# An LSTM with a residual on one core: the last block of h Wh is multiplied by halves of the columns, and the output gate's sigmoid is made by halves

## The chip, the cores and the metric

One Trainium2 chip, one of its cores. The metric is the device time of one execution in microseconds (us); lower is better. TensorE (PE in the profile) does the matrix products, with its weight loads shown apart as PEld; VectorE is DVE, ScalarE is ACT, GpSimd is POOL, and SyncE (SP) issues DMA transfers.

## The reference

An LSTM over 512 time steps for 32 sequences, with 512 inputs and 512 hidden units, in float32; its hidden states are added to its input.

```python
xW = jnp.einsum('ntd,dg->ntg', x, Wx) + b
def step(carry, xw_t):
    prev_h, prev_c = carry
    a = xw_t + prev_h @ Wh                 # [32, 2048]
    i = jax.nn.sigmoid(a[:, :Hd])
    f = jax.nn.sigmoid(a[:, Hd:2 * Hd])
    o = jax.nn.sigmoid(a[:, 2 * Hd:3 * Hd])
    g = jnp.tanh(a[:, 3 * Hd:])
    next_c = f * prev_c + i * g
    next_h = o * jnp.tanh(next_c)
    return ((next_h, next_c), next_h)
...
return x + hs
```

The products `prev_h @ Wh` depend on the step before; the products x Wx don't.

## The kernel before

**Layout.** The 2048 gate columns are cut into four groups j of 512 columns, and the 32 sequences of group j lie on partitions 32j to 32j+31. So one PSUM bank of 128 partitions by 512 columns (2 KB a partition) holds all gates of one step. Within a group the 512 columns are two halves of 256 columns, and a half holds 64 hidden units ("u" in `cell`) with their four gates. A hidden unit's gates all lie in the same half.

**One step.** `h_part(t)` adds h Wh to the step's bank `gbank[t % 2]`, into which the input part was copied before (`seed_step`, L585). The 512 rows of Wh are four blocks k of 128; for each k and each j there is one matmul of 128 x 32 weights (h of block k) by 128 x 512 columns (Wh), 16 in all. A float32 matmul is two instructions on TensorE, so the profile counts 32 for a step. `cell(t)` then makes the gates on ScalarE and the state on VectorE. For each half it computes a sigmoid of two gates (L225, 128 columns) and a tanh (L226, 64 columns); the output gate's sigmoid follows once for both halves (L227, 128 columns). VectorE makes the products (L229) and the new c (L230) of each half; ScalarE makes tanh c (L232); VectorE makes h (L234) and transposes it into the form that the next step's matmuls take as weights (L236). Blocks k = 0 and 1 of the next step need the first half of the units, and k = 2 and 3 the second.

**What stands beside it.** The x Wx of steps 24 to 503 is computed for groups of 24 steps by a fast matrix product: 20 smaller products of seven parts, that is 140 parts of 4 matmuls with 256 columns for 24 steps (`emit_matmuls`, L477). Their results are summed in `evacuate` and `w_op` on ScalarE and VectorE. These matmuls are emitted behind `h_part(t)` and fill TensorE while `cell(t)` runs; 140 parts over 24 steps makes 6 parts in 20 of the steps and 5 parts in four. For the first 20 steps, and for the last ones, plain products x Wx (`plain_block`, L159) fill in.

**The last steps.** From step 478 on (`SPLIT`), `is_split(t)` holds: the two halves of a step stand in two banks (`PAIRS`), every matmul of `h_part` is by halves of 256 columns, and `cell` goes through the halves one after the other, with an output sigmoid of 64 columns in each.

**Order.** Each engine takes its instructions in the order in which the code emits them (`manual_schedule`); a tile framework adds the waits on semaphores. Every step emits `h_part(t)`, then loads and copies, then the filling matmuls, then `cell(t)`.

Of the kernel before, what the change touches and what calls it, by code (L numbers as in the profile page):

```python
# [8 lines left out]
AF = mybir.ActivationFunctionType  # L9
# [6 lines left out]
NJ = 4  # L16
# [72 lines left out]
def kernel(  # L89
# [10 lines left out]
    nc = tc.nc  # L100
# [40 lines left out]
    def x_of(t):  # L141
        return xnat[:, xslot(t // TC), t % TC]
# [45 lines left out]
    def is_split(t):  # L188
        return t >= SPLIT

    def bank_of(t):
        if t < KEPT:
            return [gbank[0], gbank[1], xbank[3], xbank[4], xbank[0]][t]
        return gbank[t % 2]

    def half_of(t, i):
        if is_split(t):
            return PAIRS[t % 2][i][:, 0:HW]
        return bank_of(t)[:, i * HW : (i + 1) * HW]

    def h_part(t):
        if is_split(t):
            order = [(i, k) for i, ks in ((0, (0, 1)), (1, (0,)), (0, (2, 3)), (1, (1, 2, 3))) for k in ks]
        else:
            order = [(None, k) for k in range(NJ)]
        for i, k in order:
            dst = bank_of(t) if i is None else half_of(t, i)
            for j in range(NJ):
                m = wh_sb[:, k, j] if i is None else wh_sb[:, k, j, i * HW : (i + 1) * HW]
                nc.tensor.matmul(  # L210
                    dst[j * B : (j + 1) * B], state["ht"][:, k], m, start=False, stop=True, skip_group_check=True
                )

    def cell(t):
        n, tt = divmod(t, TC)
        s, nxt = sring[t % 2], sring[(t + 1) % 2]
        o = oring[0]
        ht = htr[t % 2]
        by_gate = lambda a: a.rearrange("p (h g u) -> p h g u", g=G, u=H)
        for part in [(0,), (1,)] if is_split(t) else [(0, 1)]:  # L220
            i = slice(part[0], part[-1] + 1)
            units = slice(H * part[0], H * (part[-1] + 1))
            g = by_gate(half_of(t, part[0])) if is_split(t) else by_gate(bank_of(t))
            for n_, u in enumerate(part):
                nc.scalar.activation(s[:, u, 0:2], g[:, n_, 0:2], AF.Sigmoid)  # L225
                nc.scalar.activation(s[:, u, 2], g[:, n_, 3], AF.Tanh)  # L226
            nc.scalar.activation(o[:, i], g[:, :, 2], AF.Sigmoid)  # L227
            for u in part:
                nc.vector.tensor_mul(prod[:, u], s[:, u, 0:2], s[:, u, 2:4])  # L229
                add(nxt[:, u, 3], prod[:, u, 0], prod[:, u, 1])  # L230
            for u in part:
                nc.scalar.activation(tanh_c[:, HALVES[u]], nxt[:, u, 3], AF.Tanh)  # L232
            for u in part:
                nc.vector.tensor_mul(hbuf[:, HALVES[u]], o[:, u], tanh_c[:, HALVES[u]])  # L234
                if t < T - 1:
                    nc.vector.transpose(ht[:, 2 * u : 2 * u + 2].rearrange("p q b -> p (q b)"), hbuf[:, HALVES[u]])  # L236
            if t == T - 1:
                add(tanh_c[:, units], hbuf[:, units], x_last[:, units])
                nc.sync.dma_start(out=out[n][:, tt * P + units.start : tt * P + units.stop], in_=tanh_c[:, units])
        if t == T - 1:  # L240
            return
        state["ht"] = ht
        oc = ocr[t // 2 % 2]
        (nc.gpsimd if t < T - 8 else nc.vector).tensor_add(oc[:, tt % 2], x_of(t), ht)  # L244
        if tt % 2 == 1 or t == T - 2:
            m = tt % 2 + 1
            stores.append(
                lambda: nc.sync.dma_start(
                    out=out[n][:, (tt + 1 - m) * P : (tt + 1) * P],
                    in_=oc[:, 0:m].rearrange("p t q b -> p (t q b)"),  # L250
                )
            )
            if t == T - 2:
                stores.pop()()
# [463 lines left out]
    with tc.manual_schedule():  # L718
# [57 lines left out]

        for t in range(T):
            h_part(t)
            for f in stores + kept_stores:
                f()  # L780
# [18 lines left out]
            if t < HEAD_STEPS:  # L799
# [17 lines left out]
                for i, (kind, m) in enumerate(chunks):  # L817
                    if kind == "plain":
# [4 lines left out]
                        if i == 0:  # L823
                            cell(t)
                            if t + 1 >= KEPT:
                                seed_step(t + 1)
                            flush_v()
# [6 lines left out]
                    else:  # L834
# [13 lines left out]
                        if i == 0:  # L848
                            cell(t)
                            seed_step(t + 1)  # L850
                            flush_v()
                            if t == plains_done + 1:
                                load_seeds(((0, 0), (1, 1), (2, 2)), nc.gpsimd)
# [26 lines left out]
            g = group_loaded - 1  # L880
# [11 lines left out]
            for _ in range(0 if t < SPLIT - 2 else 2 if t < SPLIT else 1):  # L892
                if plain_tail:
                    p, c = plain_tail.pop(0)
                    plain_block(HEAD + NG * GS + p, c, tail_banks[p % 2])
                    if c == 3:
                        kept_late.append(p)
            cell(t)
            for p in kept_late:
                dst = cbuf[:, take(free_c), 0:2].rearrange("p s c -> p (s c)")  # L900
# [54 lines left out]
```

## Time and profile before

| | us |
|---|---|
| median of 3 runs | 3151.49 |
| lowest and highest | 3150.75, 3151.80 |
| span of the profiled execution, first to last instruction | 3148.0 |
| median less that span (start and end around the instructions) | 3.5 |
| TensorE busy in that span | 3119.0 |
| VectorE, ScalarE, GpSimd busy | 2232.8, 1454.6, 235.6 |

The span is that of one execution under the profiler; only the span is known of it, so the 3.5 us around it is taken from the median. A timeline row gives the start, the length of a run of like instructions, the engine, the line, the tiles, the shape and the count; in brackets stand the idle time before it and what ended it. Lengths of TensorE rows reach to the modelled end of the last matmul, and matmuls overlap: the pace of TensorE is read from one row's start to the next row's start.

### The profile page before, as it was taken

The numbers are of one execution on the slowest core, as the hardware profiler recorded it, in microseconds if no ns is written. First come the engines' busy times: TensorE is split into PE (matmuls) and PEld (weight loads), VectorE is DVE, ScalarE is ACT, GpSimd is POOL, SyncE is SP. The second block draws the span as 40 slices with busy tenths as digits, with TensorE's granted clock in tenths as the row PEclk, the third lists the DMA queues.
The fourth block names the chain that finished last, engine by engine and source line by source line (L and its number), as shares of the span: only waits on it lengthen the run. The fifth ranks groups of instructions, "written<-read, shape, count | busy, mean of one in ns | idle before, by whom it ended". The sixth has DMA issues, their size and how long they took to land.

```text
span 3148.0 us, 105007 instructions
## 1 busy us (share of the span) xinstructions
PE 3119.0 (99%) x41944; PEld 1616.1 (51%) x41944; DVE 2232.8 (71%) x6217; ACT 1454.6 (46%) x5481; POOL 235.6 (7%) x511
## 2 busy tenths in 40 slices
PE   9899999999999999999999999999999999999998
PEld 6544555555555555555555555555555555555465
DVE  5687777767676777777776767777777768677644
ACT  1244444444444444444444444444444444444444
POOL 0000000000000000000000000000000000000000
PEclk9999999999999999999999999999999999999999
DMA  8888777777877777777778777777777777777831
GB/s 290 286 284 269 241 257 243 248 256 247 262 226 254 249 260 241 259 241 249 257 244 265 231 249 251 261 243 251 243 253 257 245 259 231 250 255 235 270 94 37
DMA packets 310808, 766.66 MB, mean 244 GB/s; under 512 B 49392, under 2 KB 92144, under 8 KB 309808
## 3 DMA queue, kind: packets, MB, share of 16 engines
q1 hardware_dynamic: 296800, 740.82, 71.9%
q10 hardware_dynamic: 13280, 18.35, 1.6%
q8 instruction: 331, 5.42, 0.7%
q14 instruction: 157, 1.29, 0.1%
q0 software_dynamic: 240, 0.79, 0.1%
HBM read 577.04 MB, written 182.71 MB: 241 GB/s over the span
## 4 chain that ended last, share of the span: by engine, by line
PE 94%; DVE 3%; DMA 2%; issue 1%; ACT 1%; SPq 0%; POOL 0%; DVEq 0%; ACTq 0%; POOLq 0%
PE gbank L210 52%; PE xbank L477 31%; PE bbank L477 5%; PE xbank L159 2%; PE xbank L210 2%; DVE cbuf L353 1%; PE bbank L159 1%; DMA r<-in_L_cond_Wx_dram 0%; DMA xw<-xwd 0%; DMA xs<-in_L_cond_Wx_dram 0%; DVE prod L229 0%; DVE ubuf L388 0%; DMA vring<-vdram 0%; DVE s L230 0%; DMA r<-in_L_cond_b_dram 0%
## 5 line engine op out<-in xcount | busy, mean ns | idle before, releaser
L210 PE MATMUL gbank<-wh_sb,ht 128*32 128x512 f32 (+1 forms) x16288 | 1792.7, 579 | 6.9 <-DVE ht L236 2.3
L210 PEld LDWEIGHTS gbank<-wh_sb,ht 128*32 128x32 f32 x16288 | 615.0, 110 | 905.7 <-issue 727.1
L477 PE MATMUL xbank<-vring,ubuf 128*32 128x256 f32 x14400 | 932.8, 379 | 10.7 <-DVE ubuf L388 5.9
L225 ACT ACTIVATE s<-gbank 128x128 f32<-128x128 f32 x984 | 275.9, 281 | 1291.5 <-PE gbank L210 1270.9
L477 PEld LDWEIGHTS xbank<-vring,ubuf 128*32 128x32 f32 x14400 | 560.7, 110 | 377.0 <-issue 179.1
L229 DVE TENSOR_TENSOR prod<-s 128x128 f32<-128x128 f32 x1024 | 293.8, 287 | 648.6 <-ACT s L226 648.1
L353 DVE TENSOR_TENSOR cbuf<-cbuf 128x1024 f32<-128x1024 f32 x480 | 581.2, 1218 | 3.9
L244 POOL TENSOR_TENSOR oc<-xnat,ht 128x128 f32<-128x128 f32 x504 | 233.7, 464 | 2874.3 <-DVE ht L236 1601.3
L232 ACT ACTIVATE tanh_c<-s 128x64 f32<-128x64 f32 x1024 | 262.0, 257 | 278.8 <-DVE s L230 273.6
L236 DVE STREAM_TRANSPOSE ht<-hbuf 128x64 f32<-128x64 f32 x1022 | 250.8, 245 | 74.4 <-DVE hbuf L234 0.9
L585 ACT COPY gbank<-xw 128x512 f32<-128x512 f32 x473 | 284.1, 601 | 0.1
L230 DVE TENSOR_TENSOR s<-prod 128x64 f32<-128x64 f32 x1024 | 230.2, 225 | 35.3
L523 ACT COPY cbuf<-xbank 128x512 f32<-128x512 f32 x400 | 233.8, 585 | 40.8 <-PE xbank L477 27.2
L234 DVE TENSOR_TENSOR hbuf<-o,tanh_c 128x64 f32<-128x64 f32 x1024 | 213.2, 208 | 27.2 <-ACT tanh_c L232 26.1
L226 ACT ACTIVATE s<-gbank 128x64 f32<-128x64 f32 x984 | 226.6, 230 | 0.0
L533 DVE TENSOR_TENSOR cbuf<-xbank,cbuf 128x256 f32<-128x256 f32 x400 | 164.0, 410 | 79.0 <-ACT cbuf L532 74.8
L477 PE MATMUL bbank<-vring,ubuf 128*32 128x256 f32 x2400 | 192.3, 379 | 0.6 <-DVE cbuf L529 0.6
L477 PE MATMUL xbank<-vring,xs 128*32 128x256 f32 x2400 | 172.3, 381 | 0.8 <-DVE cbuf L533 0.5
L477 PE MATMUL xbank<-vring,r 128*32 128x256 f32 x2400 | 171.6, 379 | 0.1
L529 DVE TENSOR_TENSOR cbuf<-bbank,cbuf 128x256 f32<-128x256 f32 x400 | 162.0, 405 | 2.7 <-PE bbank L477 2.7
L536 DVE TENSOR_TENSOR cbuf<-xbank,cbuf 128x256 f32<-128x256 f32 x400 | 162.5, 406 | 0.0
L539 ACT COPY cbuf<-xbank 128x256 f32<-128x256 f32 x400 | 145.3, 363 | 20.4 <-PE xbank L477 11.1
(84 smaller groups left out, 1585.4 us busy)
## 6 DMA issues: line engine op xcount, KB each, us to landing
vring<-vdram SPq DMA_DIRECT2D x340, 896.0 KB, 5.9
xwd<-cbuf SPq DMA_DIRECT2D x240, 512.0 KB, 7.1
xw<-xwd SPq DMA_DIRECT2D x1920, 64.0 KB, 3.7
out_dram<-oc SPq DMA_DIRECT2D x255, 128.0 KB, 2.8
xnat<-in_x_dram SPq DMA_DIRECT2D x63, 512.0 KB, 5.0
xs<-in_x_grouped_dram SPq DMA_DIRECT2D x10, 1536.0 KB, 10.6
vring<-vdram SPq DMA_DIRECT2D x20, 768.0 KB, 6.6
r<-in_x_grouped_dram SPq DMA_DIRECT2D x10, 1536.0 KB, 10.3
```

Source lines behind the costliest of these rows:

```text
L210: nc.tensor.matmul(dst[j * B : (j + 1) * B], state["ht"][:, k], m, start=False, stop=True, skip_group_check=True)
L225: nc.scalar.activation(s[:, u, 0:2], g[:, n_, 0:2], AF.Sigmoid)
L226: nc.scalar.activation(s[:, u, 2], g[:, n_, 3], AF.Tanh)
L229: nc.vector.tensor_mul(prod[:, u], s[:, u, 0:2], s[:, u, 2:4])
L230: add(nxt[:, u, 3], prod[:, u, 0], prod[:, u, 1])
L232: nc.scalar.activation(tanh_c[:, HALVES[u]], nxt[:, u, 3], AF.Tanh)
L236: nc.vector.transpose(ht[:, 2 * u : 2 * u + 2].rearrange("p q b -> p (q b)"), hbuf[:, HALVES[u]])
L244: (nc.gpsimd if t < T - 8 else nc.vector).tensor_add(oc[:, tt % 2], x_of(t), ht)
L353: op(c_of(dst), c_of(src), c_of(bb))
L477: nc.tensor.matmul(dst[q * B : (q + 1) * B], left_of(gr, s, r)[:, q * B : (q + 1) * B], vring[:, row % 3, RIGHT[r]], start=start, stop=Tru ...
L523: nc.scalar.copy(t[:, 0:4:3], xb.rearrange("p (n c) -> p n c", n=2))
L585: nc.scalar.copy(bank_of(t), src)
```

## The change

Two edits. In `h_part`, for all steps before the split, the last block k = 3 is no longer four matmuls of 512 columns, but eight of 256: first the first halves of the four groups j, then the second halves. All go to the same bank as before. In `cell`, the output gate's sigmoid stands inside the loop over the halves, behind the tanh of its half, with 64 columns each time. In the split steps each part holds one half, so both edits leave these as they are.

```diff
@@ h_part
         else:
-            order = [(None, k) for k in range(NJ)]
+            order = [(None, k) for k in range(NJ - 1)] + [(i, NJ - 1) for i in range(2)]
         for i, k in order:
             dst = bank_of(t) if i is None else half_of(t, i)
@@ cell
         for part in [(0,), (1,)] if is_split(t) else [(0, 1)]:
-            i = slice(part[0], part[-1] + 1)
             units = slice(H * part[0], H * (part[-1] + 1))
             g = by_gate(half_of(t, part[0])) if is_split(t) else by_gate(bank_of(t))
             for n_, u in enumerate(part):
                 nc.scalar.activation(s[:, u, 0:2], g[:, n_, 0:2], AF.Sigmoid)
                 nc.scalar.activation(s[:, u, 2], g[:, n_, 3], AF.Tanh)
-            nc.scalar.activation(o[:, i], g[:, :, 2], AF.Sigmoid)
+                nc.scalar.activation(o[:, u], g[:, n_, 2], AF.Sigmoid)
```

How the instructions stand on an engine is shown below as the built program has it. A row gives the line, the operation, the tiles with the number of their buffer, the size and how many follow each other; in brackets are the semaphores for which the first of them waits, named by the engine or DMA queue that raises them. The changed file is one line shorter, so its L224, L225, L226 and L476 are L225, L226, L227 and L477 before.

TensorE in a step in the middle of the program, before (the step's 16 matmuls, and the fill behind them):

```order
L210 MATMUL gbank_0_72<-wh_sb_76,ht_1_95 32x512 [waits DVE_49,Activation_49]
L210 MATMUL gbank_0_72<-wh_sb_76,ht_1_95 32x512 x7
L210 MATMUL gbank_0_72<-wh_sb_76,ht_1_95 32x512 [waits DVE_49]
L210 MATMUL gbank_0_72<-wh_sb_76,ht_1_95 32x512 x7
L477 MATMUL xbank_2_68<-vring_77,ubuf_78 32x256 x4
```

The same step in the changed program:

```order
L210 MATMUL gbank_0_72<-wh_sb_76,ht_1_95 32x512 [waits DVE_49,Activation_49]
L210 MATMUL gbank_0_72<-wh_sb_76,ht_1_95 32x512 x7
L210 MATMUL gbank_0_72<-wh_sb_76,ht_1_95 32x512 [waits DVE_49]
L210 MATMUL gbank_0_72<-wh_sb_76,ht_1_95 32x512 x3
L210 MATMUL gbank_0_72<-wh_sb_76,ht_1_95 32x256 x8
L476 MATMUL xbank_2_68<-vring_77,ubuf_78 32x256 x4
```

The last four matmuls of 512 columns are eight of 256; no wait is added or moved, and the fill follows as before.

ScalarE in a step in the middle of the program, before (the copy of the next step's input part, the gates, tanh c, and a copy of the fill's results):

```order
L585 COPY gbank_1_73<-xw_83 128x512 [waits DMAHW6_49,DMAHW1_49,DMAHW7_49,DMAHW0_49,Activation_49]
L225 ACTIVATE s_0_88<-gbank_0_72 128x128 [waits PE_49]
L226 ACTIVATE s_0_88<-gbank_0_72 128x64
L225 ACTIVATE s_0_88<-gbank_0_72 128x128
L226 ACTIVATE s_0_88<-gbank_0_72 128x64
L227 ACTIVATE o_0_90<-gbank_0_72 128x128 [waits DVE_49]
L232 ACTIVATE tanh_c_92<-s_1_89 128x64 [waits DVE_49,Activation_49] x2
L532 COPY cbuf_75<-xbank_0_66 128x256 [waits PE_49]
```

The same place in the changed program:

```order
L584 COPY gbank_1_73<-xw_83 128x512 [waits DMAHW6_49,DMAHW1_49,DMAHW7_49,DMAHW0_49,Activation_49]
L224 ACTIVATE s_0_88<-gbank_0_72 128x128 [waits PE_49]
L225 ACTIVATE s_0_88<-gbank_0_72 128x64
L226 ACTIVATE o_0_90<-gbank_0_72 128x64 [waits DVE_49]
L224 ACTIVATE s_0_88<-gbank_0_72 128x128
L225 ACTIVATE s_0_88<-gbank_0_72 128x64
L226 ACTIVATE o_0_90<-gbank_0_72 128x64 [waits DVE_49]
L231 ACTIVATE tanh_c_92<-s_1_89 128x64 [waits DVE_49,Activation_49] x2
L531 COPY cbuf_75<-xbank_0_66 128x256 [waits PE_49]
```

One output sigmoid has moved up between the halves, and there is one instruction more. The first sigmoid of the step waits for TensorE; the sigmoid of the second half (the second L224) has no wait of its own in either program.

ScalarE in a split step, the same in both programs (rows of the program before):

```order
L225 ACTIVATE s_0_88<-xbank_0_66 128x128 [waits PE_49]
L226 ACTIVATE s_0_88<-xbank_0_66 128x64
L227 ACTIVATE o_0_90<-xbank_0_66 128x64
L232 ACTIVATE tanh_c_92<-s_1_89 128x64 [waits DVE_49]
L225 ACTIVATE s_0_88<-xbank_1_67 128x128 [waits PE_49]
```

Nothing moved here: the halves lie in two banks (`xbank_0` and `xbank_1`), and the sigmoid of each half waits for TensorE by itself.

## The prediction

> **What bounds the kernel now.** I read the page's shares and its chain first, then a timeline of TensorE alone, then one of all engines over a single step.
>
> ```profile
> span 3148.0 us, 105007 instructions
> PE 3119.0 (99%) x41944; PEld 1616.1 (51%) x41944; DVE 2232.8 (71%) x6217; ACT 1454.6 (46%) x5481; POOL 235.6 (7%) x511
> PE 94%; DVE 3%; DMA 2%; issue 1%; ACT 1%; SPq 0%; POOL 0%; DVEq 0%; ACTq 0%; POOLq 0%
> PE gbank L210 52%; PE xbank L477 31%; PE bbank L477 5%; PE xbank L159 2%; PE xbank L210 2%; DVE cbuf L353 1%; PE bbank L159 1%; DMA r<-in_L_cond_Wx_dram 0%; DMA xw<-xwd 0%; DMA xs<-in_L_cond_Wx_dram 0%; DVE prod L229 0%; DVE ubuf L388 0%; DMA vring<-vdram 0%; DVE s L230 0%; DMA r<-in_L_cond_b_dram 0%
> ```
>
> TensorE is the bound, and L210, the line that is edited, is the largest piece of the chain. But "99% busy" hides something: a matmul's row lasts beyond the start of the next, so a short wait between two matmuls doesn't show as idle. The distance from one step's first L210 matmul to the next step's shows it:
>
> ```profile
> 1535.94 3.64 PE L210 MATMUL gbank<-wh_sb,ht 128*32 128x512 f32 x32
> 1539.37 1.51 PE L477 MATMUL xbank<-vring,ubuf 128*32 128x256 f32 x24
> 1540.67 0.64 PE L477 MATMUL bbank<-vring,ubuf 128*32 128x256 f32 x8
> 1541.10 0.64 PE L477 MATMUL xbank<-vring,ubuf 128*32 128x256 f32 x8
> 1541.72 3.64 PE L210 MATMUL gbank<-wh_sb,ht 128*32 128x512 f32 x32
> 1545.15 1.07 PE L477 MATMUL xbank<-vring,ubuf 128*32 128x256 f32 x16
> ...
> 1547.74 3.64 PE L210 MATMUL gbank<-wh_sb,ht 128*32 128x512 f32 x32
> ...
> 1571.84 3.64 PE L210 MATMUL gbank<-wh_sb,ht 128*32 128x512 f32 x32
> ```
>
> Five steps from 1541.72 to 1571.84 take 30.12 us, 6.024 each: 3.43 for L210 (1541.72 to 1545.15) and 2.59 for 48 fill instructions, with no gap. These long steps are bound by TensorE's pace. The step from 1535.94 to 1541.72 has only 40 fill instructions. They start at 1539.37, the last 8 at 1541.10, and 8 take 0.43 (1540.67 to 1541.10), so TensorE could go on at 1541.53; it goes on at 1541.72. In these short steps the cell comes 0.19 us too late. By the code 4 of 24 steps are short; of the 458 steps 20 to 477 that is about 76.
>
> What the wait in a short step consists of, in another one of the same kind:
>
> ```profile
> 1503.26 1.50 PE L477 MATMUL xbank<-vring,ubuf 128*32 128x256 f32 x24
> 1503.53 0.28 ACT L225 ACTIVATE s<-gbank 128x128 f32<-128x128 f32 x1 [2.35 <-PE gbank L210]
> 1503.70 0.22 ACT L226 ACTIVATE s<-gbank 128x64 f32<-128x64 f32 x1
> 1503.81 0.28 ACT L225 ACTIVATE s<-gbank 128x128 f32<-128x128 f32 x1
> 1503.95 0.29 DVE L229 TENSOR_TENSOR prod<-s 128x128 f32<-128x128 f32 x1 [0.77 <-ACT s L226]
> 1503.96 0.24 ACT L226 ACTIVATE s<-gbank 128x64 f32<-128x64 f32 x1
> 1504.07 0.31 ACT L227 ACTIVATE o<-gbank 128x128 f32<-128x128 f32 x1
> 1504.28 0.22 DVE L230 TENSOR_TENSOR s<-prod 128x64 f32<-128x64 f32 x1
> 1504.42 0.28 DVE L229 TENSOR_TENSOR prod<-s 128x128 f32<-128x128 f32 x1
> 1504.60 0.26 ACT L232 ACTIVATE tanh_c<-s 128x64 f32<-128x64 f32 x1 [0.22 <-DVE s L230]
> 1504.74 0.23 DVE L230 TENSOR_TENSOR s<-prod 128x64 f32<-128x64 f32 x1
> 1504.89 0.23 DVE L234 TENSOR_TENSOR hbuf<-o,tanh_c 128x64 f32<-128x64 f32 x1
> 1505.22 0.25 DVE L236 STREAM_TRANSPOSE ht<-hbuf 128x64 f32<-128x64 f32 x1
> 1505.61 0.64 PE L210 MATMUL gbank<-wh_sb,ht 128*32 128x512 f32 x4
> ```
>
> The first half's chain runs sigmoid, tanh, products, new c, tanh c, h, transpose (done at 1505.47), and 0.14 later the next L210 starts. The second half's transpose comes later, but is needed only by block k = 2, half of 3.43 us after. The output sigmoid isn't on this chain: it ends at 1504.38, and ScalarE then idles 0.22 until tanh c can start.
>
> A few long steps are late for another reason. VectorE is still in its sums (L353) when the gates are ready:
>
> ```profile
> 1519.85 2.48 DVE L353 TENSOR_TENSOR cbuf<-cbuf 128x1024 f32<-128x1024 f32 x2
> 1521.53 0.22 ACT L226 ACTIVATE s<-gbank 128x64 f32<-128x64 f32 x1
> 1522.24 0.28 DVE L229 TENSOR_TENSOR prod<-s 128x128 f32<-128x128 f32 x1
> 1523.90 0.64 PE L210 MATMUL gbank<-wh_sb,ht 128*32 128x512 f32 x4
> ```
>
> The tanh is done at 1521.75, but the product starts at 1522.24. Gates that are ready sooner would not help there.
>
> **Edit 1, the halves of block k = 3.** Each of the 478 steps before the split loses 4 matmuls of 512 columns and gains 8 of 256: 8 instructions less, 16 more, and as many weight loads. The columns are the same, so the question is what the cut itself costs. The split steps at the end run the whole of h Wh by halves, and the trace has both forms a few steps apart:
>
> ```profile
> 2985.93 3.64 PE L210 MATMUL gbank<-wh_sb,ht 128*32 128x512 f32 x32 [0.37 <-ACT xbank L583]
> 2989.36 0.41 PE L159 MATMUL xbank<-xs,xnat 128*32 128x256 f32 x2
> ...
> 2996.31 3.66 PE L210 MATMUL gbank<-wh_sb,ht 128*32 128x256 f32 x64
> 2999.76 1.10 PE L159 MATMUL xbank<-xs,xnat 128*32 128x256 f32 x16
> ...
> 3014.21 3.66 PE L210 MATMUL gbank<-wh_sb,ht 128*32 128x256 f32 x64
> 3017.66 1.10 PE L159 MATMUL xbank<-xs,xnat 128*32 128x256 f32 x16
> ```
>
> Whole: 2989.36 - 2985.93 = 3.43 us. By halves: 2999.76 - 2996.31 = 3.45, and 3.45 again from 3014.21. All 16 matmuls cut cost 0.02 us, so the 4 that are cut here cost a quarter, 0.005 us a step, and 478 x 0.005 = 2.4 us. With starts rounded to 0.01 the difference is 0.00 to 0.04, so the bounds are 0 and 4.8 us. I take the middle, since the two split steps agree. It is paid in full: in long steps TensorE is the bound, in short ones the chain starts at the last matmul of L210, which ends later by the same 0.005.
>
> The Trainium skill, page "TensorE: Matmul & The Clock Gate", section "Wait — 56ns, not 53.3ns?", has a fixed cost of about 2.5 ns for each matmul. Charged to each of the 8 added instructions it would be 20 ns a step and 9.6 us in all. The trace disagrees with that count: 32 added instructions cost 20 ns there, 0.6 ns each, so by the rows the sum stays at 2.4.
>
> Does the first half's sigmoid start earlier? That would be worth 0.19 us in each short step. But ScalarE's rows in the changed program show one wait on TensorE, at the step's first sigmoid, and none at the second half's. Since the second half must not be read before its last matmul, the first wait has to cover all 16. In the split steps, with a bank for each half, both sigmoids wait for themselves. So I count no earlier start.
>
> **Edit 2, the output sigmoid by halves.** ScalarE makes one instruction more a step. Its rows overlap: after a 64-column function the next starts 0.11 us later (1503.70 to 1503.81, 1503.96 to 1504.07), though it lasts 0.22. The first output sigmoid now stands ahead of the second half's gates, so the second tanh, which ended at 1503.96 + 0.24 = 1504.20, ends at 1504.31. VectorE takes its product no sooner than 1504.42, because it is behind the first half's L229 and L230; with the 0.03 from a function's end to the product (1503.70 + 0.22 to 1503.95) it could have started at 1504.34. The delay lies under VectorE's own work, with 0.08 left. Without that cover it would go on: product, new c (1504.74), and behind it in VectorE's order the first half's h (1504.89) and transpose, for which TensorE waits. ScalarE's own end moves from 1504.38 to about 1504.41, under the 0.22 idle before tanh c. The wait on VectorE that the output sigmoid carries is for the h of the step before, long done; the copies and evacuations queued behind tanh c keep their times. I take zero; bounds below.
>
> What price could the added function have? A separate 64-column output sigmoid is a row of this trace only in the split steps:
>
> ```profile
> L227 ACT ACTIVATE o<-gbank 128x128 f32<-128x128 f32 x475 | 146.4, 308 | 0.0
> L227 ACT ACTIVATE o<-gbank 128x64 f32<-128x64 f32 x34 | 7.8, 230 | 0.0
> ```
>
> From below it is the 0.11 from start to start, from above its whole 0.23 laid end to end. With 0.23 the second product could start at 1504.46, 0.04 late, and 76 short steps would lose 3.0 us; long steps have the 0.19 that short ones lack, and more. I take 0.11, since four neighbouring rows show it.
>
> **The sum.** Span 3148.0 + 2.4 = 3150.4; with the 3.5 us around it (3151.49 - 3148.0) the time is 3153.9 us, 0.08% over the median before. Nothing else moves: DMAs, VectorE's and GpSimd's rows are the same. With edit 2 at its bounds the sum goes from 3151.5 (0 and 0) to 3159.3 (4.8 and 3.0).
>
> **Rivals.**
>
> *The halves do overlap.* If ScalarE started on the first half while TensorE made the second, the chain would begin two groups of halves, 0.43 us, sooner and short steps would lose their 0.19: 76 x 0.19 = 14.4 us off, 3139.5 us. For it: that is how the split steps work. Against it: the missing second wait. The steps held by L353 would gain nothing. 4%.
>
> *The added sigmoid blocks ScalarE.* The second half's gates are pushed by more than the 0.19 that the second product has to spare (1504.20 + 0.03 to 1504.42), and then VectorE's order passes the delay to the first half's transpose. With the whole 0.31 of the wide form it is 0.12 a short step, 9.1 us, and 3163.0 us: slower. It decides from a push of 0.19 on; over 0.2% slower it is from about 0.24. Against it: the starts 0.11 apart. 6%. The Trainium skill, page "ScalarE: Activation LUTs", section "Rules for kernel authors", budgets about 0.3 us for an ACTIVATE and 0.83 ns an element, 0.35 us here; by that 0.16 a short step, some 3166 us. The start distances in the trace are a third of it.
>
> *Each added matmul instruction pays by itself.* If the cut costs 2.5 ns (0.02 us over the 8 added groups of four) for every instruction and not for a group of four, it is 20 ns a step: 3161.1 us. The split steps speak against it, but there the halves lie in two banks, and here in one. 3%.
>
> **How the numbers follow.** The forecast has 83%, the rivals 4, 6 and 3%, and 4% stay for something that I don't see, split between both sides. About 0.2%, 6.3 us, is what a measurement of this kernel can tell from no change; the forecast lies within it. Faster by more: 4% and a part of the rest, 0.05. Slower by more: most of the second rival, the third, and a part of the rest, 0.11. Within: 0.84. The range goes from 3150.5, a little below the sum with both costs at zero, since single runs differ by 0.7 about the median, to 3159.0, next to the sum with both at their upper bounds; outside are the first and third rivals and most of the second.
>
> **What would show it.** In a long step L210 should take some 3.435 us from its first matmul to the first fill matmul, and long steps 6.03 instead of 6.024. The first sigmoid should follow the last half matmul, not the first four pairs: its idle row still ends with TensorE some 0.27 after the first fill row. Short steps should stay near 5.78 and the second L229 some 0.89 behind the first L225 (1503.53 to 1504.42). The prediction is wrong if short steps fall to 5.6 (overlap), if the second L229 moves back (ScalarE's price), or if long steps grow by 0.02 or more (TensorE's).

## The result and the profile after

The changed kernel takes 3155.36 us, the median of 12 runs (3151.39 to 3158.14); the kernel before takes 3153.18, the median of 12 runs beside it (3150.75 to 3157.02). The ratio is 1.0004 with a 95% interval of 0.9996 to 1.0013, that is 1.3 us faster to 4.1 us slower. No change in the time can be told, and the 2.4 us that were forecast lie within the interval. What the edits did is read from the traces, where a step's length is good to some 0.01 us.

The page after, its span, shares and the chain by engine:

```profile
span 3152.4 us, 113133 instructions
PE 3122.3 (99%) x45768; PEld 1773.7 (56%) x45768; DVE 2232.0 (71%) x6217; ACT 1484.4 (47%) x5959; POOL 234.9 (7%) x511
PE 95%; DVE 2%; DMA 2%; issue 1%; ACT 1%; SPq 0%; POOL 0%; ACTq 0%; DVEq 0%; POOLq 0%
```

TensorE has 3824 instructions more, which are 478 x 8, and ScalarE 478. TensorE's busy time grew by 3.3 us, ScalarE's by 29.8.

The span is 4.4 us longer than before, but 1.9 of that was lost before the first edited instruction. The first L210 matmul, in the timeline of TensorE, stands at 25.52 before and at 27.43 after; the plain products ahead of it started late and slowly in this execution. Rows of both timelines, before and then after, show where the rest is (the first split step is the row of 64 instructions):

```profile
25.52 3.81 PE L210 MATMUL gbank<-wh_sb,ht 128*32 128x512 f32 x32
```

```profile
27.43 3.70 PE L210 MATMUL gbank<-wh_sb,ht 128*32 128x512 f32 x40
...
1538.77 3.65 PE L210 MATMUL gbank<-wh_sb,ht 128*32 128x512 f32 x40
1542.21 1.50 PE L476 MATMUL xbank<-vring,ubuf 128*32 128x256 f32 x24
...
1544.56 3.65 PE L210 MATMUL gbank<-wh_sb,ht 128*32 128x512 f32 x40
1547.99 1.07 PE L476 MATMUL xbank<-vring,ubuf 128*32 128x256 f32 x16
...
1574.70 3.65 PE L210 MATMUL gbank<-wh_sb,ht 128*32 128x512 f32 x40
...
2996.21 3.66 PE L210 MATMUL xbank<-wh_sb,ht 128*32 128x256 f32 x64 [0.45 <-DVE hbuf L233]
```

The five long steps that began at 1541.72 before begin at 1544.56 here and take 30.14 us, 6.028 each against 6.024. The short step ahead of them takes 5.79 (1538.77 to 1544.56) against 5.78. The first split step began at 2991.80 before and begins at 2996.21 now: 4.41 later, of which 1.91 are from the start. So the 478 edited steps cost 2.50 us.

The cell of a short step after the change, which answers to the one shown of before:

```profile
1506.34 0.28 ACT L224 ACTIVATE s<-gbank 128x128 f32<-128x128 f32 x1 [2.36 <-PE gbank L210]
1506.52 0.22 ACT L225 ACTIVATE s<-gbank 128x64 f32<-128x64 f32 x1
1506.62 0.23 ACT L226 ACTIVATE o<-gbank 128x64 f32<-128x64 f32 x1
1506.72 0.30 ACT L224 ACTIVATE s<-gbank 128x128 f32<-128x128 f32 x1
1506.88 0.26 ACT L225 ACTIVATE s<-gbank 128x64 f32<-128x64 f32 x1
1506.98 0.27 ACT L226 ACTIVATE o<-gbank 128x64 f32<-128x64 f32 x1
1507.24 0.28 DVE L228 TENSOR_TENSOR prod<-s 128x128 f32<-128x128 f32 x1
1507.41 0.26 ACT L231 ACTIVATE tanh_c<-s 128x64 f32<-128x64 f32 x1 [0.16 <-DVE s L229]
...
1508.42 0.64 PE L210 MATMUL gbank<-wh_sb,ht 128*32 128x512 f32 x4
```

The first sigmoid still waits for the whole of h Wh. The added output sigmoid pushes the second half by 0.10 us, and the second product stands 0.90 behind the first sigmoid (1506.34 to 1507.24), against 0.89 before. The tanh it needs ends at 1507.14, so 0.07 of cover are left after the 0.03 between engines. ScalarE's idle before tanh c shrinks from 0.22 to 0.16.

### The profile page after: what moved, and what is told of

It reads as the page before. It is cut to its first block, busy times and chain, and to the rows that moved or that the text cites. A ratio compares the mean times of both kernels' runs of the same rounds, so it can differ in the third digit from the quotient of the medians.

```text
span 3152.4 us, 113133 instructions
## 1 busy us (share of the span) xinstructions
PE 3122.3 (99%) x45768; PEld 1773.7 (56%) x45768; DVE 2232.0 (71%) x6217; ACT 1484.4 (47%) x5959; POOL 234.9 (7%) x511
## 4 chain that ended last, share of the span: by engine, by line
PE 95%; DVE 2%; DMA 2%; issue 1%; ACT 1%; SPq 0%; POOL 0%; ACTq 0%; DVEq 0%; POOLq 0%
PE gbank L210 53%; PE xbank L476 32%; PE bbank L476 5%; PE xbank L159 2%; PE xbank L210 2%; DMA vring<-vdram 1%; PE bbank L159 1%; DVE cbuf L352 1%; DMA r<-in_L_cond_b_dram 0%; PE gbank L159 0%; DVE ubuf L387 0%; DVE prod L228 0%; DVE s L229 0%; DMA r<-in_L_cond_Wx_dram 0%; DMA vdram<-vring 0%
## 5 line engine op out<-in xcount | busy, mean ns | idle before, releaser
L210 PE MATMUL gbank<-wh_sb,ht 128*32 128x512 f32 (+1 forms) x20088 | 1795.2, 501 | 6.1 <-DVE ht L235 2.3
L210 PEld LDWEIGHTS gbank<-wh_sb,ht 128*32 128x32 f32 x20088 | 766.9, 110 | 957.5 <-issue 726.9
L476 PE MATMUL xbank<-vring,ubuf 128*32 128x256 f32 x14400 | 933.4, 380 | 11.9 <-DVE ubuf L387 6.5
L224 ACT ACTIVATE s<-gbank 128x128 f32<-128x128 f32 x984 | 282.9, 287 | 1296.7 <-PE gbank L210 1292.4
L476 PEld LDWEIGHTS xbank<-vring,ubuf 128*32 128x32 f32 x14400 | 562.0, 110 | 229.4 <-DVE ubuf L387 7.5
L226 ACT ACTIVATE o<-gbank 128x64 f32<-128x64 f32 x984 | 247.5, 251 | 0.0
L225 ACT ACTIVATE s<-gbank 128x64 f32<-128x64 f32 x984 | 234.2, 238 | 0.0
L476 PE MATMUL bbank<-vring,ubuf 128*32 128x256 f32 x2400 | 192.6, 380 | 0.6 <-DVE cbuf L528 0.6
L476 PE MATMUL xbank<-vring,xs 128*32 128x256 f32 x2400 | 172.4, 381 | 0.8 <-DVE cbuf L532 0.5
L476 PE MATMUL xbank<-vring,r 128*32 128x256 f32 x2400 | 171.6, 379 | 0.1
```

What stands on the lines that cost most here:

```text
L210: nc.tensor.matmul(dst[j * B : (j + 1) * B], state["ht"][:, k], m, start=False, stop=True, skip_group_check=True)
L226: nc.scalar.activation(o[:, u], g[:, n_, 2], AF.Sigmoid)
L476: nc.tensor.matmul(dst[q * B : (q + 1) * B], left_of(gr, s, r)[:, q * B : (q + 1) * B], vring[:, row % 3, RIGHT[r]], start=start, stop=Tru ...
```

## The experiments

Each kernel was compared with the kernel before on the same chip, and steps were measured from one step's first h Wh matmul to the next step's. "Late" means a step more than 20 ns over the median of its kind, counted over steps 30 to 469.

### The two edits apart

`halves_only` keeps the first edit and makes the output sigmoid whole; `sigmoid_only` keeps the second and leaves block k = 3 whole.

```diff
 halves_only, against the changed kernel
+            i = slice(part[0], part[-1] + 1)
...
-                nc.scalar.activation(o[:, u], g[:, n_, 2], AF.Sigmoid)
+            nc.scalar.activation(o[:, i], g[:, :, 2], AF.Sigmoid)
 sigmoid_only, against the changed kernel
-            order = [(None, k) for k in range(NJ - 1)] + [(i, NJ - 1) for i in range(2)]
+            order = [(None, k) for k in range(NJ)]
```

> Edit 1 alone: block k = 3 by halves, the output sigmoid whole as before. Theory (the cut costs TensorE about 5 ns a step, the output sigmoid nothing): long and short steps 5 ns longer than before, 6.028 and 5.786 us, as in the changed kernel, and the time 1 to 3 us over the kernel before. Rival (part of the changed kernel's cost is the second output sigmoid): steps shorter than the changed kernel's, nearer to 6.023 and 5.781.

> Edit 2 alone: block k = 3 with 512 columns as before, the output sigmoid by halves. Theory: long and short steps as before, 6.023 and 5.781 us, the second L229 about 0.89 us behind the step's first sigmoid as before, the time within 0.1% of the kernel before. Rival (the added sigmoid delays the second half): the second L229 0.04 us or more later and short steps 5.82 us or more, the time 3 to 9 us over the kernel before.

| kernel | ratio to before | 95% interval | long step, median (us) | late long steps of 367 | steps 24 to 460, against before (us) |
|---|---|---|---|---|---|
| before | | | 6.023 | 66 | |
| changed | 1.0004 | 0.9996 to 1.0013 | 6.028 | 57 | +0.90 |
| `halves_only` | 1.0013 | 1.0004 to 1.0022 | 6.028 | 66 | +2.38 |
| `sigmoid_only` | 0.9996 | 0.9987 to 1.0005 | 6.023 | 57 | -1.16 |

The halves cost 5 ns a step (2.38 us over 436 steps), and the sigmoid adds nothing to an undisturbed step. The time of `halves_only` is some 4 us over before, a little more than the 1 to 3 expected; the 2.38 of the trace lie in that range. But the sigmoid isn't neutral: it takes away some late steps and gives 1.2 us back. The nine steps fewer are mostly ones that were 0.03 to 0.05 late, at the same places in both programs with the old ScalarE order and at none in the two with the new one. One of them is step 54. Its first half's new c and the tanh c behind it, in the kernel before and then in `sigmoid_only`:

```profile
447.05 0.22 DVE L230 TENSOR_TENSOR s<-prod 128x64 f32<-128x64 f32 x1
447.64 0.44 ACT L232 ACTIVATE tanh_c<-s 128x64 f32<-128x64 f32 x2 [0.50 <-DVE prod L229]
```

```profile
447.65 0.22 DVE L229 TENSOR_TENSOR s<-prod 128x64 f32<-128x64 f32 x1
447.97 0.26 ACT L231 ACTIVATE tanh_c<-s 128x64 f32<-128x64 f32 x1 [0.16 <-DVE s L229]
```

The tanh starts 0.37 us behind the end of its new c before, and 0.10 in `sigmoid_only`. In the kernel before, ten of the 908 tanh c of steps 24 to 477 are late like this, by 0.28 to 0.29 us, and no other by more than 0.05. Counted through ScalarE's records in the trace from 0, their numbers are 575, 831, 1087, 1343 and so on: all leave 63 when divided by 128, and no other tanh c does. With one instruction more a step, no tanh c falls on such a number in `sigmoid_only` or the changed kernel, and none is late. In `sums_capped` (below), which has the old ScalarE order in a shifted list, five fall there, in other steps, and these five are late. Eight of the ten make eight of the nine late long steps; one makes a short step 0.30 us late; and one, at the end of step 88, makes step 89 late by 0.49 instead of 0.21. Together that is some 0.9 of the 1.2 us. So most of the gain came from which instruction happens to stand at these places, not from the sigmoid's halves as such. Why ScalarE is late there is open.

### What a cut costs

`all_halves` cuts all four blocks; `last_quarters` cuts block k = 3 into pieces of 128 columns.

```diff
 all_halves, against the changed kernel
-            order = [(None, k) for k in range(NJ - 1)] + [(i, NJ - 1) for i in range(2)]
+            order = [(i, k) for k in range(NJ) for i in range(2)]
 last_quarters, against the changed kernel
-            order = [(None, k) for k in range(NJ - 1)] + [(i, NJ - 1) for i in range(2)]
+            order = [(None, k) for k in range(NJ - 1)] + [(i, NJ - 1) for i in range(4)]
...
-            dst = bank_of(t) if i is None else half_of(t, i)
+            cw = HW if is_split(t) else HW // 2
+            cols = slice(0, W) if i is None else slice(i * cw, (i + 1) * cw)
+            dst = half_of(t, i) if is_split(t) else bank_of(t)[:, cols]
...
-                m = wh_sb[:, k, j] if i is None else wh_sb[:, k, j, i * HW : (i + 1) * HW]
+                m = wh_sb[:, k, j, cols]
```

> The changed kernel with all four blocks k by halves in the steps before the split, in the order first halves of k = 0, second halves of k = 0, and so on: four times the cut, 16 matmuls. Theory (2.5 ns for each added group of four instructions): h Wh of a step takes 3.453 us against 3.433 before, long steps 6.043 us, the time 6 to 10 us over the kernel before. Rival (each instruction pays 2.5 ns by itself): h Wh 80 ns longer, 3.51 us, and 38 us over the kernel before.

> The changed kernel with block k = 3 by quarters of 128 columns instead of halves, 16 matmuls for it. Theory (a fixed 2.5 ns for each group of four instructions): 8 groups instead of 4, h Wh 3.448 us, 15 ns over the kernel before, the time 5 to 7 us over it. Rival (below some width the weight loads bind: four loads are a row of about 0.16 to 0.20 us in the trace, a quarter's group lasts 0.11): each of the 8 groups takes 0.16 to 0.20 instead of 0.11, h Wh 0.4 to 0.75 us longer, and the time 190 to 360 us over the kernel before.

Starts of the steps in `all_halves`, and the first fill matmul behind one h Wh:

```profile
1548.75 3.66 PE L210 MATMUL gbank<-wh_sb,ht 128*32 128x256 f32 x64
1552.20 1.07 PE L476 MATMUL xbank<-vring,ubuf 128*32 128x256 f32 x16
...
1578.96 3.66 PE L210 MATMUL gbank<-wh_sb,ht 128*32 128x256 f32 x64
```

And in `last_quarters`:

```profile
1546.32 3.66 PE L212 MATMUL gbank<-wh_sb,ht 128*32 128x512 f32 x56
1549.76 1.07 PE L478 MATMUL xbank<-vring,ubuf 128*32 128x256 f32 x16
...
1576.50 3.66 PE L212 MATMUL gbank<-wh_sb,ht 128*32 128x512 f32 x56
```

`all_halves`: 3.45 us for h Wh, and five steps from 1548.75 to 1578.96 in 30.21, 6.042 each; the median over all steps is 3.453 for h Wh, 20 ns more than 3.433. `last_quarters`: five steps in 30.18, 6.036 each, and a median h Wh of 3.448, 15 ns more. So each added group of four instructions costs 2.5 ns, in one bank as in two, and down to 128 columns: the quarters' eight groups take 3.448 - 6 x 0.429 = 0.874 us, 0.109 each, and the weight loads don't bind. Both rivals fall. The times are 1.0042 (1.0028 to 1.0055) and 1.0016 (1.0007 to 1.0025); `all_halves` lost 8.56 us over steps 24 to 460, as 436 x 0.020 says, and the rest of its 14 us (6 to 10 were expected) lies around them. Most of that rest is in step 475, at the end of the fill, which takes 12.68 us against 9.18 before; the longest wait there is for a load of `vring`, and that step's length differs by microseconds between all these traces.

### How much room the second half has on ScalarE

Two kernels make the first half's output sigmoid two and four times in a row. That proved a poor measure: a repeat writes the same buffer, so in the built program it waits for the one before. Two more kernels write the extra sigmoids to a spare buffer.

```diff
 sigmoid_twice (4 instead of 2: sigmoid_four_times), against the changed kernel
-                nc.scalar.activation(o[:, u], g[:, n_, 2], AF.Sigmoid)
+                for _ in range(2 if u == 0 and not is_split(t) else 1):
+                    nc.scalar.activation(o[:, u], g[:, n_, 2], AF.Sigmoid)
 spare_two (one fp32 tile and one pass in spare_one), against the changed kernel
+    spare = work.tile([P, 2, H], mybir.dt.bfloat16, name="spare")
                 nc.scalar.activation(o[:, u], g[:, n_, 2], AF.Sigmoid)
+                if u == 0 and not is_split(t):
+                    for r in range(2):
+                        nc.scalar.activation(spare[:, r], g[:, n_, 2], AF.Sigmoid)
```

> The changed kernel with the first half's output sigmoid made twice in a row in the steps before the split (the second writes the same values again). Theory (each pushes the second half's gates by 0.10 to 0.11 us, and the second L229 has 0.19 to spare before the change): two pushes make 0.21, so the second L229 comes 0.02 us later and short steps take about 5.80 us; long steps as in the changed kernel, 6.028. Rival (a function costs its whole 0.23 us): short steps 6.0 us.

> The changed kernel with the first half's output sigmoid made four times in a row in the steps before the split. Theory: four pushes make 0.42 us, the second L229 is 0.23 later, short steps take about 6.01 us; long steps have 0.24 between the transpose and TensorE's turn, so they stay near 6.03; the time some 17 to 20 us over the kernel before. Rival (the cover is larger than read): short steps stay at 5.79 us and the time at the changed kernel's.

> The changed kernel with one more 64-column sigmoid of the first half's output gate in the steps before the split, written to a buffer that nothing reads, behind the first half's output sigmoid; unlike a repeat into the same buffer it waits for nothing. Theory (an ACTIVATE that waits for nothing pushes the next by 0.10 us, and after the change some 0.07 us of cover are left): the second L229 and short steps 0.03 us later, 5.82 us; long steps 6.028. Rival (each added function costs 0.25 us, as in the runs with repeats): short steps 5.97 us.

> As with one spare sigmoid, but two of them, to two places of a bfloat16 buffer that nothing reads. Theory (0.10 us each, 0.07 us of cover): short steps 0.14 us longer than the changed kernel's, 5.92 us, long steps 6.028 as before; the time 8 to 12 us over the changed kernel. Rival (0.25 us each): short steps 6.22 us, and long steps 6.22 too.

In `sigmoid_four_times` the four sigmoids of one step are one row of 1.00 us, 0.25 each; a short step (1507.14 to 1513.62) and a long one (1513.62 to 1520.10) take the same:

```profile
1507.14 3.65 PE L210 MATMUL gbank<-wh_sb,ht 128*32 128x512 f32 x40 [0.24 <-DVE hbuf L234]
...
1511.12 1.00 ACT L227 ACTIVATE o<-gbank 128x64 f32<-128x64 f32 x4
```

```profile
1513.62 3.65 PE L210 MATMUL gbank<-wh_sb,ht 128*32 128x512 f32 x40 [0.24 <-DVE hbuf L234]
1520.10 3.65 PE L210 MATMUL gbank<-wh_sb,ht 128*32 128x512 f32 x40 [0.24 <-DVE hbuf L234]
```

All steps are 6.48 us, and the time is 1.0706 of before (1.069 to 1.0722). With two, short steps take 5.97 and the ratio is 1.0091 (1.0077 to 1.0105). The expected 5.80 and 6.01 were missed, because they were reckoned with 0.10 a push; with 0.25 for each added one, less the 0.07 of cover, they come out (5.79 + 0.18 and 5.79 + 0.68). Long steps with four, expected near 6.03, were bound by the cell too. The rival of `sigmoid_twice`, 6.0, came near, but a push by a function's whole length is not what the next two kernels show.

With the spare buffer, a short step of `spare_two` (the first halves' functions, then the second half's):

```profile
1514.86 3.65 PE L211 MATMUL gbank<-wh_sb,ht 128*32 128x512 f32 x40
1518.56 0.28 ACT L225 ACTIVATE s<-gbank 128x128 f32<-128x128 f32 x1 [2.36 <-PE gbank L211]
...
1518.94 0.36 ACT L230 ACTIVATE spare<-gbank 128x64 bf16<-128x64 f32 x2
1519.15 0.33 ACT L225 ACTIVATE s<-gbank 128x128 f32<-128x128 f32 x1
...
1519.62 0.29 DVE L232 TENSOR_TENSOR prod<-s 128x128 f32<-128x128 f32 x1
...
1520.81 0.64 PE L211 MATMUL gbank<-wh_sb,ht 128*32 128x512 f32 x4
```

Two pushes are 0.21 (1518.94 to 1519.15). The second product is 1.06 behind the first sigmoid, 0.16 later than in the changed kernel, and the step takes 5.95 against 5.79, 0.16 longer: the cover that was left is some 0.05 to 0.07, as read. With one spare sigmoid short steps have a median of 5.832, 0.046 longer. Undisturbed long steps stay at 6.028 in both. The ratios, 1.0035 (1.0022 to 1.0049) and 1.0096 (1.0082 to 1.011), are larger than the short steps alone make, since long steps that VectorE holds grow too (late time in long steps 12.4 and 19.7 us, against 9.2 in the changed kernel). So the time expected of `spare_two`, 8 to 12 us over the changed kernel, was missed: over steps 24 to 460 it is 23.

### A bank for each half

`crossed_banks` gives each half a bank of its own without needing another: the first half of a step in one bank's first columns, the second in the other bank's last columns, exchanged at each step. The rows left out pick each half's bank in `cell` and copy the input part by halves (`seed_half`) in place of the whole copy; the last block's cut in the first 24 steps is gone too.

```diff
 crossed_banks, against the changed kernel
+    def is_crossed(t):
+        return HEAD <= t < SPLIT
     def half_of(t, i):
...
+        if is_crossed(t):
+            return gbank[(t + i) % 2][:, i * HW : (i + 1) * HW]
     h_part:
+        elif is_crossed(t):
+            order = [(i, k) for i in range(2) for k in range(NJ)]
         else:
-            order = [(None, k) for k in range(NJ - 1)] + [(i, NJ - 1) for i in range(2)]
+            order = [(None, k) for k in range(NJ)]
...
     cell, behind the first half's output sigmoid and behind the second tanh c:
+                if u == 0 and is_crossed(t) and is_crossed(t + 1):
+                    seed_half(t + 1, 1)
+                if u == 1 and is_crossed(t + 1):
...
+                    seed_half(t + 1, 0)
```

> The changed kernel with the two halves of a step in two banks in steps 24 to 477: the first half in one bank's first columns, the second half in the other bank's last columns, the banks changing places each step; all matmuls by halves, first half first; the input part is copied by halves, each when its columns are free. Theory (the first half's gates start early only when its bank is its own; the cell is late in short steps alone): the first sigmoid starts while TensorE makes the second half, some 1.7 us before its end; short steps are bound by TensorE, about 5.61 us against 5.786; long steps 6.043 us, 20 ns longer than before; together 3 to 7 us under the kernel before. Rival (VectorE, whose sums stand ahead of the cell, is what sets the cell's start anyway): short steps stay near 5.78 us and the time is 5 to 10 us over the kernel before.

The ratio is 0.9958 (0.9945 to 0.997), 3139.35 us against 3151.41: faster than both. A short step, then rows of a long step that was late before, and last the first rows of that step in the kernel before:

```profile
1530.98 3.71 PE L217 MATMUL gbank<-wh_sb,ht 128*32 128x256 f32 x64
...
1533.07 0.28 ACT L232 ACTIVATE s<-gbank 128x128 f32<-128x128 f32 x1 [1.20 <-PE gbank L217]
...
1534.73 0.28 ACT L232 ACTIVATE s<-gbank 128x128 f32<-128x128 f32 x1 [0.75 <-PE gbank L217]
...
1536.60 0.69 PE L217 MATMUL gbank<-wh_sb,ht 128*32 128x256 f32 x8
```

```profile
1512.86 3.71 PE L217 MATMUL gbank<-wh_sb,ht 128*32 128x256 f32 x64
1513.19 0.42 DVE L546 TENSOR_TENSOR cbuf<-xbank,cbuf 128x256 f32<-128x256 f32 x1 [0.78 <-ACT cbuf L545]
...
1514.86 2.48 DVE L366 TENSOR_TENSOR cbuf<-cbuf 128x1024 f32<-128x1024 f32 x2
...
1517.25 0.28 DVE L238 TENSOR_TENSOR prod<-s 128x128 f32<-128x128 f32 x1
...
1518.90 0.47 PE L217 MATMUL gbank<-wh_sb,ht 128*32 128x256 f32 x4
```

```profile
1517.65 3.64 PE L210 MATMUL gbank<-wh_sb,ht 128*32 128x512 f32 x32
1518.17 0.42 DVE L533 TENSOR_TENSOR cbuf<-xbank,cbuf 128x256 f32<-128x256 f32 x1 [0.52 <-ACT cbuf L532]
```

The first sigmoid starts 2.09 us into h Wh and 1.66 before the second half's. Two things differ here from the changed kernel: the banks, and that the whole first half is made first, which is why the lead is 1.66 and not the 0.43 of one block. The second order alone, in one bank, was not tried. Short steps take 5.62 us here (median 5.612), bound by TensorE. Long ones take 6.043 with the cost of the cut, and five are late. Over steps 30 to 469 the short steps gave 12.7 us, and the long ones 1.9, since 9.2 us less of late time outweighs 7.3 for the cut. The gain is larger than expected because the late long steps went too. The step that starts at 1512.86 is the one from 1517.65 to 1523.90 before. VectorE still makes two sums ahead of its product, yet the product starts 4.39 into the step instead of 4.59 (1517.65 to 1522.24). VectorE's first evacuation waits for a copy on ScalarE that stands behind the cell's tanh c; a cell that ends sooner lets that copy and all that follows start sooner, at 0.33 into the step (1512.86 to 1513.19) instead of 0.52 (1517.65 to 1518.17). The opposite change agrees: in `spare_two` the cell ends some 0.16 later, and the steps that VectorE held are 0.17 longer than before.

### Late steps and the uneven fill

`sums_capped` starts no further sum (L353) with less than 800 ns of VectorE's allowance left, `even_fill` counts the fill in single matmuls, and `crossed_capped` joins the cap to the crossed banks.

```diff
 sums_capped, against the kernel before; crossed_capped, against crossed_banks
-            while wqueue and room["dve"] > 300:
+            while wqueue and room["dve"] > 800:
 even_fill, against the kernel before
-            target = min(R * 7 * 4 + (t + 1 - STREAM0) * R * 7 // GS * 4, 4 * len(items))
+            target = min(R * 7 * 4 + (t + 1 - STREAM0) * R * 7 * 4 // GS, 4 * len(items))
...
-            after = max(0, min(R * 7 * 4 + (t + 2 - STREAM0) * R * 7 // GS * 4, 4 * len(items)) - pos[0])
+            after = max(0, min(R * 7 * 4 + (t + 2 - STREAM0) * R * 7 * 4 // GS, 4 * len(items)) - pos[0])
```

> The kernel before, with the planner starting no further sum of 1024 columns (L353) on VectorE in a step when less than 800 ns of its allowance are left, instead of 300: the work ahead of the cell is at most about 3.9 us in a step instead of 4.7. Theory (the regularly late long steps, 0.21 and 0.08 us, are late because VectorE is still in its sums when the gates are ready): these disappear, long steps stay at 6.02 us on the mean too, short steps stay at 5.78; the time 8 to 11 us under the kernel before. Rival (they are late for another reason that returns every 24 steps, a load or a store): they stay, and the time is that of the kernel before.

> The kernel before, with the fill of each step counted in single matmuls instead of parts of four: 23 or 24 matmuls (46 or 48 instructions) in each step instead of 20 or 24. Theory (the cell is 0.19 us late in the 76 steps with 20 matmuls, and in a step with 23 it is in time): all steps are bound by TensorE, 5.92 to 6.03 us, and the time 10 to 14 us under the kernel before. Rival (a part's four matmuls run side by side, and one cut in two by h Wh loses this): each cut costs up to 0.1 to 0.2 us, no gain or a loss of up to 60 us.

> The kernel with the crossed banks and the same cap on VectorE's sums. Theory (with the banks crossed the cell has time enough, and no regular late step is left): within 0.1% of the crossed kernel, long steps 6.043 and short ones 5.612 us. Rival (VectorE's sums still hold some of its steps, or the cap moves work to where it hurts): more than 3 us under or over it.

`sums_capped`: 0.9971 (0.996 to 0.9982), 3143.3 us against 3153.08. Seven long steps are late instead of 66, and the mean is 6.024, as its theory had it. The cap has a price. In one short step of 7.48 us ScalarE's copy waits for a store to free its buffer, and the cell behind it is late:

```profile
924.37 0.58 ACT L523 COPY cbuf<-xbank 128x512 f32<-128x512 f32 x1 [4.40 <-DMA xwd<-cbuf]
...
927.45 0.64 PE L210 MATMUL gbank<-wh_sb,ht 128*32 128x512 f32 x4 [1.68 <-DVE hbuf L234]
```

Six short steps lost 3.8 us in this way. With the crossed banks the cap only costs: 0.9973 (0.9962 to 0.9984), medians 5.612 and 6.043 as without it, but 12 short steps late by 6.6 us together. Its expectation, within 0.1% of `crossed_banks`, failed, and the rival that the cap moves work to where it hurts came true.

`even_fill`: 1.0045 (1.0032 to 1.0057), slower, and the expected 10 to 14 us don't come. By TensorE's pace a step of 3.433 and 23.3 fill matmuls at 0.108 would take 5.95 us; the mean of steps 24 to 460 is 6.033. The start of a step behind a cut part, from the first half's transpose to the first sigmoid:

```profile
1542.84 0.24 DVE L236 STREAM_TRANSPOSE ht<-hbuf 128x64 f32<-128x64 f32 x1
1543.24 0.59 PE L210 MATMUL gbank<-wh_sb,ht 128*32 128x512 f32 x1
1543.30 0.39 PE L477 MATMUL xbank<-vring,xs 128*32 128x256 f32 x3
1543.52 3.61 PE L210 MATMUL gbank<-wh_sb,ht 128*32 128x512 f32 x31
1547.19 0.28 ACT L225 ACTIVATE s<-gbank 128x128 f32<-128x128 f32 x1 [2.30 <-PE gbank L210]
```

One instruction of h Wh starts beside the last three of the fill, and the other 31 start 0.28 us later. So the first sigmoid comes 3.95 us into the step (1543.24 to 1547.19); the median over steps 30 to 469 is 3.94, against 3.70 before, and the cell ends later by as much. In 417 of the 440 steps from 30 to 469 the next h Wh starts within 0.16 us of the end of the first half's transpose, which is the mark of a late cell; before, it was 138, the short steps and the late long ones. The fill keeps its pace, four instructions every 0.22 us. So the time is lost at the end of h Wh, and with it in the cell. The loss lies in the rival's range, but not for its reason, that a cut part's matmuls no longer run side by side.

## Why the prediction was right

**The bound.** Right: long steps by TensorE, short ones by the cell. The "few" long steps that VectorE holds were more than that sounds: 56 of the 66 late ones before have their product right behind a sum (L353). `spare_two` lengthens short steps by what it adds to the cell and leaves undisturbed long ones alone.

**Edit 1, 0.005 us a step.** Right: h Wh went from 3.433 to 3.438 us, and `halves_only` lost 2.38 us in 436 steps. The rule of a fixed cost for every matmul, as the rival put it, fell with `all_halves`: 32 added instructions cost 20 ns, in one bank.

**"It is paid in full."** Not quite. The long steps that VectorE holds don't pay: their length is set by its sums, and TensorE's 5 ns go into the wait. Without step 89, 53 late steps return every 24 steps; on the mean they took 0.2 ns longer in the changed kernel than before, and 3.5 ns less in `halves_only`. At 5 ns each that is worth only some 0.3 us. Over steps 30 to 469 the long ones of the changed kernel grew by 2.44 ns on the mean, half of their undisturbed 5; most of the missing half is edit 2's, the late tanh c that are gone.

**Edit 2, zero.** Right for undisturbed steps, with 0.07 us of cover left where 0.08 were read. As a term of the sum it was some 1.2 us off, to the good (`sigmoid_only`, in one trace of each kernel). The prediction let what stands behind the cell keep its times and so missed that one instruction more shifts all of ScalarE's list, and with it the tanh c that are late at certain places.

**The sum.** 2.4 us were forecast, and the trace has 2.50 between the first edited step and the first split one. The agreement is in part luck: steps 24 to 460 cost only 0.90, and the steps around them 1.6, some of it in waits for loads that differ from run to run. The measured times alone, with an interval from 1.3 us faster to 4.1 slower, tell neither the 2.4 nor its terms.

**The rivals.** That the halves don't overlap in one bank was right: the first sigmoid came no sooner. With a bank each, in `crossed_banks`, they did overlap. The prediction's step that failed stands in this rival: that the steps held by L353 would gain nothing from an earlier cell. They did, since the cell's end also sets when VectorE's next sums start. That the rival's 3139.5 us and the 3139.35 of `crossed_banks` agree is chance: the rival had neither the cut of all blocks nor the late long steps in its sum. The added sigmoid pushes by 0.10, not by its length, as forecast; it would be 0.25 if it waited for the one before it.

## What to carry to other kernels

To let a reader start on half of a result, look at the waits, not at the order of the products: here halves in one bank shared one wait, and the split cost 5 ns a step for nothing; halves in two banks, with the whole first half made first, started 1.7 us apart and made the kernel 0.4% faster. Each bank is one tile of the framework here, so the runs don't show which of the two ties the halves together. When an engine reads 99% busy, measure a step from start to start, and sort the steps by how much they have to do: the short ones showed the wait that the busy time hid. Before a stall is called out of reach of an edit, ask what starts the work that causes it: it may begin where the edited chain ends. And before a gain of a microsecond is put down to what an edit means, look at whether it merely moved instructions to other places.

## What the runs showed of the hardware that was not expected

A 64-column sigmoid on ScalarE held the next function back by 0.10 us when nothing tied them, and by 0.25 when it wrote the buffer of the one before and waited for it. A tanh c whose number among ScalarE's records left 63 when divided by 128 came 0.28 us late, ten of ten in the kernel before and none of the 898 others. On TensorE four matmul instructions of 128 columns side by side, with their four weight loads, took 0.109 us, so cutting 512 columns into quarters cost no more than 2.5 ns for each added group of four.
